# Four graph layers on one core: where an eigenproblem's last steps, a normalization pass and the first loads stand in the order of work

## The chip, the core and the metric

The kernel runs on one core of a Trainium2 chip. The core has five engines, each with its own queue of instructions, which it works off in order: TensorE (PE; its weight loads are listed apart as PEld), VectorE (DVE), ScalarE (ACT), GpSimd (POOL) and SyncE (SP), which here only issues DMAs. ScalarE and POOL issue some DMAs too. Engines wait for one another through semaphores. The metric is the device time of one execution in microseconds; lower is better.

## The reference

The input x is 128 graphs of 64 nodes with 256 features, in float32. Four layers follow, each as `x = layernorm(x + layer(x))`, and all with one 64 x 64 adjacency matrix.

```
layer 0: h = relu(adj @ (x @ Wg0 + bg0)); h = relu(adj @ (h @ Wg1 + bg1))
         for p in 1..4: LSTM over windows of p nodes, its last state replaces the window's last node
layer 1: A_hat = D^-1/2 (adj + I) D^-1/2; z = (A_hat @ x) @ W1.T + b1
         z = relu(batchnorm(z)); z = z @ W2.T + b2; batchnorm(z) over all 8192 nodes
layer 2: e = a . leaky_relu(Xq[src] + Xq[dst]) + log(adj[src,dst] + eps) for 512 edges, 4 heads
         softmax over the edges of each source node; Y[src] += attn * Xv[dst]; Y @ W_out.T
layer 3: _, U = eigh(L_norm(adj)); h = relu((U.T @ x) @ W1 + b1); U @ (h @ W2 + b2)
```

The eigenvectors U depend on the adjacency alone, so they can be worked out at any time before layer 3.

## The kernel before

**Data.** x stays in SBUF as the tile X: 64 blocks of 128 rows (two graphs) by 256. Products with the adjacency use a 128 x 128 matrix with the 64 x 64 one twice on its diagonal: `bda` (adjacency), `bdah` (layer 1's A_hat). Layer 3 writes its U and U transposed into these same two tiles (`bdu`, `bdut`), by `spread()` (L2014).

**The order of work.** The program is written with Python generators that yield between steps, so that one stage's steps can be traced between those of another (`run`, L1984). A planner then orders every engine's queue: it takes instructions by the order in which they were traced, as soon as its cost model has their inputs and memory ready, and so moves some of them forward or back.

**The eigenproblem** is done mostly on VectorE in small instructions, cut into pieces (`FastEigh.steps`, L1174): tridiagonalization of the 64 x 64 matrix (62 columns, five pieces each, L733), 30 implicit QL sweeps on four 16 x 16 leaves at once, postprocessing of the sweeps on tiles of 64 x 480, rotations, then two merges (32, then 64 wide), each with a bisection of 31 bits, and the products that give U and UT. Every piece yields a number, its price. `pump(n)` (L1363) adds n to what is owed, and issues pieces until their prices have used it up (a bare yield counts 2.6). It is called after every gate of the LSTMs with 0.8 or 1.6 x M/512 x PACE (M columns; PACE is 1.75, L1361), with 6 and 5 after each block of layer 1's two passes, and with `work[0]` after each step of layer 2's scores. Before layer 2 only the QL part must be done (L1751); the remaining pieces are issued after the scores (L2022).

**The general path.** The quick eigensolver flags cases that it can't treat in `bad`. A check (L2026, L2027) turns the flag into a count of 0 or 1, and a loop over that count (L2031) holds a slower, general solver. With these inputs the loop's body is skipped, but every engine loads the count into a register and branches. In the old order this stands between the scores and layer 3.

**Layer 0** takes four groups of 16 blocks of X. `convolve` (L1520) makes the two graph convolutions of a group; `windows` (L1559) the LSTMs for p = 1 to 4; `residual` (L1610) adds and normalizes. The steps of the next group's convolution and the last group's residual are traced between the gates. Loads: identity, adjacency and constants first (L1272 to L1278), x by `load_x` (four blocks of X a DMA), then weights and biases on ScalarE's queue (L1487 to L1501).

**Layer 1** passes three times over 16 quarters of four blocks. The first pass makes z and its statistics; the second the second product and its statistics, into Y; the last (`last_pass`, L1754) scales Y, transposes it back on TensorE, adds it to X and normalizes. The last pass is traced within layer 2's scores: four steps of it ahead, then one with each step of the scores.

**Layer 2.** `scores` has 32 steps of two blocks. A step holds, for each of two heads' halves c, four edge products (L1876), their copy by ScalarE (L1882) and leaky relu by VectorE (L1883), the products with `a` (L1829), and also the maps to Xq and Xv (L1853) of the next step and the transposes (L1842) of the one after. The 16 steps of a half fill one PSUM pair `sc`. Then `softmax` (L1897) works on it on VectorE, with one exponential on ScalarE, in seven steps; `table` (L1917) transposes the result and scatters it into `attn_d` in DRAM with four indirect DMAs on POOL; `fetch` (L1932) gathers it back as dense matrices `M2` with eight DMAs on SyncE. `values` (L1965) has 33 steps: load a block pair's table from M2 (`load`, ScalarE copy L1944, POOL fetch of Xv L1947), mix (L1959), map and normalize (L1980). Steps from the 16th on need the second table.

**Layer 3.** `blocks` (L2107) is a pipeline of four stages over 16 quarters: `basis` (L2071; it also adds a constant to X on POOL), `first_map`, `back` and `second_map` (L2098; it normalizes, and stores to the output from SyncE). It needs U and the quarter's X from the values.

Of the kernel before, what the change touches and what calls it, by code (L numbers as in the profile page):

```python
# [7 lines left out]
F32 = mybir.dt.float32  # L8
I32 = mybir.dt.int32
# [5 lines left out]
N = 64  # L15
NB = 128
D = 256
# [685 lines left out]
class FastEigh(Eigh):  # L703
# [29 lines left out]
    def tridiagonal(self, A0, QT, e, dcol):  # L733
# [12 lines left out]
        for i in range(N - 2):  # L746
# [11 lines left out]
            yield 1.2  # L758
            self.rsqrt(y, h)
            yield 1.2  # L760
# [12 lines left out]
            yield 1.2  # L773
            ps = self.ps(N)
            self.mm(ps, A, H)
            yield 1.2
# [4 lines left out]
            yield 1.2  # L781
# [478 lines left out]
def tile_adj_resnorm(ctx: ExitStack, tc: tile.TileContext, I: dict, out: bass.AP, layers: int = 4):  # L1260
# [5 lines left out]
    def load(name, shape, src, eng=nc.sync, dtype=F32):  # L1266
        t = const.tile(shape, dtype, tag=name, name=name)
        eng.dma_start(t, src)
        return t


    ident = load("ident", [P, P], I["ident"])  # L1272
    bda = const.tile([P, P], F32, tag="bda", name="bda")
    v.memset(bda, 0.0)
    for b in range(2):
        nc.sync.dma_start(bda[b * N : (b + 1) * N, b * N : (b + 1) * N], I["adjT"])
    adj = load("adj", [N, N], I["adj"], s)
    cst = load("cst", [N, CONST_COLS], I["consts"], nc.gpsimd)  # L1278
    X = const.tile([P, NT, D], F32, tag="X", name="X")
    xt = I["x"].rearrange("(t b) n d -> (b n) t d", b=2)  # L1280
    kio = lambda w: w.rearrange("(k p) f -> p k f", p=P)
# [35 lines left out]
    def psum(rows, w):  # L1317
        return eps.tile([P, 512], F32, tag="eps", name="eps")[:rows, :w]
# [42 lines left out]
    PACE = 1.75  # L1361
# [98 lines left out]
    with tc.tile_pool(name="lw", bufs=1) as lw, tc.tile_pool(  # L1460
# [10 lines left out]
        def load_x(g):  # L1471
            for q in range(TG // 4):
                t0 = g * TG + q * 4
                nc.sync.dma_start(X[:, t0 : t0 + 4, :], xt[:, t0 : t0 + 4, :])
# [12 lines left out]
        wg0 = lw.tile([P, 2, D], F32, tag="wg0", name="wg0")  # L1487
        s.dma_start(wg0, kio(I["Wg0"]))
        wg1 = lw.tile([P, 2, D], F32, tag="wg1", name="wg1")
        s.dma_start(wg1, kio(I["Wg1"]))  # L1490
        bl = lw.tile([P, 4, 8], F32, tag="bl", name="bl")
        bh = lw.tile([P, 4, 8], F32, tag="bh", name="bh")
        s.dma_start(bl, I["bih"])
        s.dma_start(bh, I["bhh"])
# [3 lines left out]
        b0c = lw.tile([P, 2], F32, tag="b0c", name="b0c")  # L1498
        s.dma_start(b0c, I["bg0"].rearrange("o (c p) -> p (o c)", p=P))
        b2c = lw.tile([P, D], F32, tag="b2c", name="b2c")  # L1500
        s.dma_start(b2c, I["bg1"].partition_broadcast(P).rearrange("p o d -> p (o d)"))  # L1501
# [249 lines left out]
    while not fast.ql_done:  # L1751
        next(pieces)

    def last_pass():  # L1754

        ln = Norm(nc, sy, X, 8, act=True)
        for q in range(NQ):
            y = sy.tile([P, 2, 512], F32, tag="y", name="y")
            for c in range(2):
                s.activation(y[:, c, :], Y[:, q, c, :], AF.Identity,  # L1760
                             bias=sh2[:, c : c + 1], scale=sc2[:, c : c + 1])
            for j in range(0, 4, 2):
                ps = pp.tile([P, 512], F32, tag="m", name="m")
                for i in range(2):
                    for c in range(2):
                        te.transpose(ps[:, i * D + c * P : i * D + (c + 1) * P], y[:, c, (j + i) * P : (j + i + 1) * P], ident)
                ln.add(q * 4 + j, ps, 2)
            yield

    only1.close()  # L1770
    qlp.close()
    own.close()
    sy = own1(keep1, name="l1z", bufs=2)
# [4 lines left out]
    with ExitStack() as l2:  # L1778
# [7 lines left out]
        fast.psum, fast.bank = pp, "m"  # L1786
# [24 lines left out]
        taken, late, work = [], [], [3.5]  # L1811
# [24 lines left out]
        def transposed(k):  # L1836

            xT = []
            for t in (2 * k, 2 * k + 1):
                ps = pp.tile([P, 512], F32, tag="m", name="m")  # L1840
                for c in range(2):
                    te.transpose(ps[:, c * P : (c + 1) * P], X[:, t, c * P : (c + 1) * P], ident)  # L1842
                xT.append(sx.tile([P, 2, P], F32, tag="xT", name="xT"))
                v.tensor_copy(xT[-1].rearrange("p c n -> p (c n)"), ps[:, :D])  # L1844
            return xT

        def maps(k, xT):

            xq, xv = [], sx.tile([P, 2, D], F32, tag="xv", name="xv")
            for i in range(2):  # L1850
                ps = pp.tile([P, 512], F32, tag="m", name="m")
                for c in range(2):
                    te.matmul(ps, xT[i][:, c, :], wqv[:, c, :], start=(c == 0), stop=(c == 1))  # L1853
                xq.append(sx.tile([P, D], F32, tag="xq", name="xq", bufs=4))
                taken.append(s.copy(xq[i], ps[:, :D]))
                s.copy(xv[:, i, :], ps[:, D:])
            nc.sync.dma_start(xvd[k], xv)
            return xq

        def scores():  # L1860
# [8 lines left out]
            for k in range(K):  # L1869
                xn = None  # L1870
                for c in range(2):
# [17 lines left out]
                    if c == 1 and k < K - 2:  # L1889
                        xT = transposed(k + 2)  # L1890
                xq = xn
                pump(work[0])
# [91 lines left out]
        def run(*steps):  # L1984
            for x in steps:
                next(x, None)

        bank = None
        sc_, p3 = scores(), last_pass()
        run(*[p3] * 4)  # L1990
        work[0] = 0.0
        run(*[sc_, p3] * (NQ - 4))
        for _ in p3:
            pass
        keep1.close()
        lw, sm = own1(valuing, name="l2w", bufs=1), own1(valuing, name="l2s", bufs=2)
# [3 lines left out]
        run(*[sc_] * (HU - NQ + 4))  # L2000
        for _ in range(3):
            run(sc_, soft[0], soft[0])
        run(soft[0])
        work[0] = 4.5
        run(sc_)
# [3 lines left out]
        run(*[sc_] * 7)  # L2009
        run(sc_, val, sc_, sc_, val, sc_)  # L2010
        scoring.close()


        def spread():  # L2014
            for bd, m in ((bdu, U), (bdut, UT)):
                for b in range(2):
                    r = slice(b * N, (b + 1) * N)
                    v.tensor_copy(bd[r, r], m[r, :])

        with tc.tile_pool(name="eps3", bufs=1, space=PSUM) as eps:  # L2020
            fast.psum, fast.bank = eps, "eps"
            for _ in pieces:  # L2022
                pass
            again = ek.tile([1, 1], I32, tag="again", name="again")
            ps = psum(1, 1)
            te.matmul(ps, fast.bad, ones[:N, 0:1], start=True, stop=True)  # L2026
            v.tensor_scalar(again, ps, 0.0, None, ALU.is_gt)  # L2027
            for bd in (bdu, bdut):
                v.memset(bd, 0.0)
            spread()  # L2030
            with tc.For_i(0, nc.values_load(again[0:1, 0:1], min_val=0, max_val=1)):  # L2031
                with tc.tile_pool(name="gk2", bufs=1) as gk2, tc.tile_pool(name="gt2", bufs=1) as gt2, tc.tile_pool(
                    name="gp2", bufs=1, space=PSUM
                ) as gp2:
                    Eigh(tc, gk2, gt2, gp2, cst, ident, ones).from_leaves(*fast.state, U, UT)
                spread()
# [4 lines left out]
        with tc.tile_pool(name="l3w", bufs=1) as l3w, tc.tile_pool(name="l3s", bufs=2) as s3, tc.tile_pool(  # L2041
# [75 lines left out]
            run(val, soft[1], val, soft[1], soft[1], val, soft[1], val, soft[1], soft[1], val)  # L2117
            table(es[1])
            run(val)
            constants()  # L2120
            run(val)
            fetch(1)
            run(*[val] * 7)

            run(*[val, val, l3, val, l3] * 5)
# [64 lines left out]
```

## Time and profile before

| | us |
|---|---|
| median of three runs | 2501.85 (2501.39 to 2501.97) |
| profiled execution | 2496.09 |
| its span, first to last instruction | 2494.2 |
| TensorE busy | 2292.2 |
| VectorE busy | 1796.8 |
| ScalarE busy | 952.6 |
| layer 0's first convolution starts at | 23.7 |
| layer 0's last LSTM matmul ends at about | 1507 |
| layer 1's second pass ends on TensorE at | 1796.8 |
| last score product ends at | 2224.0 |
| the loop's register loads at | 2269.9 |
| second table landed at | 2331.9 |

The profile shows one execution; its span is what its instructions cover. Times in it are counted from its first instruction. In rows of groups, a line is `line engine operation output<-inputs shapes xcount | busy, mean ns | idle before it and what ended that`. L numbers are those of the code before. The helper lines L117 to L148 are the eigenproblem's small instructions. "Granted clock" is the share of full speed that TensorE's clock had.

### The profile page before, as it was taken

To read this page: it belongs to the slowest core of one execution; us is meant where nothing else is said; L and a number is where in the kernel's file an instruction comes from. 1 tells how busy PE (TensorE), PEld (TensorE's weight loads), DVE (VectorE), ACT (ScalarE), POOL (GpSimd) and SP (SyncE) were. 2 spreads that over 40 slices of the span, in tenths; PEclk is the share of its full clock that TensorE was granted. 3 is DMA by queue.
4 is the path that set the end of the run, shared out by engine and by line. 5 is a ranking of instruction groups with operands and counts; after the bars stand their busy time and mean duration, and the time that the engine had idled before them with its cause. 6 is when DMAs were issued, how large, how long until landed. Compare 5 with 4: busy or idle time off the path is not lost. (4 is left out here: it accounts for less than half of the span.)

```text
span 2494.2 us, 29191 instructions
## 1 busy us (share of the span) xinstructions
PE 2292.2 (92%) x9016; PEld 1225.4 (49%) x9016; DVE 1796.8 (72%) x8156; ACT 952.6 (38%) x1635; POOL 76.3 (3%) x115
## 2 busy tenths in 40 slices
PE   6999999999999999999999997989889888965797
PEld 4544654444664445655446544544433322324697
DVE  3566655677677798777888777877866676886477
ACT  1233222333222333222433222334366654544575
POOL 0000000000000000000000000000000000001232
PEclk9999999999999999999999998999999999987899
DMA  6000000001000001000101000022100005002522
GB/s 211 18 17 34 1 34 1 34 34 51 1 34 1 34 34 51 1 34 1 51 17 51 35 1 34 1 97 85 51 30 21 17 26 97 22 30 58 104 82 85
DMA packets 59859, 101.24 MB, mean 41 GB/s; under 512 B 5136, under 2 KB 40080, under 8 KB 59440
## 3 DMA queue, kind: packets, MB, share of 16 engines
q1 hardware_dynamic: 54304, 88.39, 10.9%
q0 software_dynamic: 3216, 10.21, 1.4%
q8 instruction: 72, 1.18, 0.2%
q10 hardware_dynamic: 2176, 0.72, 0.1%
q14 instruction: 91, 0.75, 0.1%
HBM read 67.84 MB, written 31.46 MB: 40 GB/s over the span
## 5 line engine op out<-in xcount | busy, mean ns | idle before, releaser
L1583 PE MATMUL pq<-H,wi 128*128 128x512 f32 (+1 forms) x2016 | 827.6, 546 | 3.8 <-DVE H L1608 3.8
L1589 ACT ACTIVATE gate<-pq,bl 128x512 f32<-128x512 f32 (+1 forms) x504 | 318.4, 635 | 835.8 <-PE pq L1587 651.2
L1583 PEld LDWEIGHTS pq<-H,wi 128*128 128x128 f32 x2016 | 372.0, 190 | 329.8 <-issue 260.2
L1587 PE MATMUL pq<-lh,wh 128*128 128x512 f32 (+1 forms) x1152 | 467.4, 533 | 14.8 <-DVE lh L1604 14.1
L1587 PEld LDWEIGHTS pq<-lh,wh 128*128 128x128 f32 x1152 | 215.5, 190 | 215.9 <-issue 141.0
L1883 DVE SCALAR_TENSOR_TENSOR xs<-xs 128x512 f32<-128x512 f32 x256 | 166.0, 681 | 84.1 <-ACT xs L1882 83.8
L1882 ACT COPY xs<-l 128x512 f32<-128x512 f32 x256 | 137.3, 589 | 108.9 <-PE l L1876 56.0
L1876 PE MATMUL l<-edge_s,xq 64*128 64x512 f32 x512 | 138.2, 657 | 24.1 <-ACT xs L1882 12.4
L1853 PE MATMUL m<-wqv,xT 128*128 128x512 f32 x256 | 126.0, 621 | 1.9 <-DVE xT L1844 1.9
L1729 PE MATMUL ps<-at,w 128*128 128x512 f32 x256 | 117.2, 610 | 9.9 <-ACT at L1725 8.8
L1746 PE MATMUL ps<-h,w 128*128 128x512 f32 x256 | 112.1, 600 | 8.8 <-ACT h L1741 8.8
L142 DVE COPY AQR<-eps 64x192 f32<-64x192 f32 (+1 forms) x125 | 35.1, 280 | 118.1 <-PE eps L148 117.9
L1253 ACT ACTIVATE X<-X,ln_sh,ln_rs 128x256 f32<-128x256 f32 x192 | 98.6, 589 | 36.6 <-DVE ln_sh L1249 28.6
L1601 ACT ACTIVATE gate<-lc 128x1024 f32<-128x1024 f32 (+1 forms) x72 | 69.0, 958 | 102.3 <-DVE lc L1596 52.2
L1237 DVE BATCH_NORM_STATS2 ln_st<-X 128x6 f32<-128x256 f32 x256 | 97.9, 413 | 1.5
L1876 PEld LDWEIGHTS l<-edge_s,xq 64*128 64x128 f32 x512 | 47.0, 196 | 84.5 <-issue 35.8
L1746 PEld LDWEIGHTS ps<-h,w 128*128 128x128 f32 x256 | 49.0, 193 | 70.4 <-issue 57.5
L1947 POOL DMA_DIRECT2D xr<-xv x32 | 17.6, 550 | 2088.2 <-DVE xs L1883 1823.4
L1729 PEld LDWEIGHTS ps<-at,w 128*128 128x128 f32 x256 | 47.9, 193 | 67.1 <-issue 49.4
L1853 PEld LDWEIGHTS m<-wqv,xT 128*128 128x128 f32 x256 | 45.4, 194 | 71.0 <-issue 57.5
L1234 DVE TENSOR_TENSOR X<-ps,X 128x512 f32<-128x512 f32 x63 | 42.8, 680 | 46.8 <-PE ps L1980 32.1
L1598 DVE TENSOR_TENSOR gate<-gate 128x1024 f32<-128x1024 f32 (+1 forms) x36 | 38.1, 1058 | 52.5 <-ACT gate L1589 52.4
(558 smaller groups left out, 3228.3 us busy)
## 6 DMA issues: line engine op xcount, KB each, us to landing
wi<-in_WihT_dram SPq DMA_DIRECT2D x16, 1024.0 KB, 4.8
wh<-in_WhhT_dram SPq DMA_DIRECT2D x12, 1024.0 KB, 6.9
X<-in_x_dram SPq DMA_DIRECT2D x16, 512.0 KB, 8.5
xd<-X SPq DMA_DIRECT2D x16, 512.0 KB, 2.6
X<-xd SPq DMA_DIRECT2D x16, 512.0 KB, 3.2
xv<-xv SPq DMA_DIRECT2D x32, 256.0 KB, 2.0
xr<-xv POOLq DMA_DIRECT2D x32, 256.0 KB, 2.9
M<-attn_d SPq DMA_DIRECT2D x16, 512.0 KB, 11.6
```

The lines of the kernel that those rows point to most:

```text
L1237: nc.vector.bn_stats(st, self.X[:, k, :])
L1253: nc.scalar.activation(x, x, AF.Identity, bias=sh[:, k : k + 1], scale=rs[:, k : k + 1])
L1583: te.matmul(ps, wi[:, kk, o * P : (o + 1) * P], at(kk, k), start=(kk == 0), stop=(k == 0 and kk == 1))
L1587: te.matmul(ps, wh[:, kk, o * P : (o + 1) * P], hst[:, kk, :M], start=False, stop=(kk == 1))
L1589: s.activation(gates[gt][:, c, :M], ps, AF.Tanh if gt == 2 else AF.Sigmoid, bias=bl[:, p - 1, o : o + 1])
L1601: s.activation(gg, cs2, AF.Tanh)
L1729: te.matmul(ps, w1[:, k, c * P : (c + 1) * P], at[:, k, :], start=(k == 0), stop=(k == 1))
L1746: te.matmul(ps, w2[:, k, c * P : (c + 1) * P], h[:, k, :], start=(k == 0), stop=(k == 3))
L1853: te.matmul(ps, xT[i][:, c, :], wqv[:, c, :], start=(c == 0), stop=(c == 1))
L1876: mms.append(te.matmul(pl[i][:, b, :], xq[i][r, c * P : (c + 1) * P], GG[r, :], start=True, stop=True))
L1882: taken.append(s.copy(x, pl[i][:, b, :]))
L1883: ready.append(v.scalar_tensor_tensor(x, x, 0.2, x, ALU.mult, ALU.max))
```

## The change

1. The general path's check and loop, with `spread`, move from behind the scores to behind layer 1's second pass, ahead of the last pass and of layer 2. All remaining pieces are now issued before it (`for _ in pieces`). So that fewer remain, PACE is 1.9 and all five of the tridiagonalization's pieces are priced 1.1 (the first row of the diff, five times). The scores no longer pump pieces.
2. The last pass works in half quarters (two blocks), normalizes four blocks at once instead of eight, and is stepped from within `scores`, twice a step. Four half quarters are traced ahead of the scores.
3. `transposed` uses one PSUM tile and one SBUF tile (a single buffer) for both blocks of a step.
4. Seven steps of the values are traced with the last seven steps of the scores (before: two in the last six). Layer 3's blocks are traced from the second softmax on, between its steps and those of the values; before, from 16 steps of the values on.
5. The adjacency halves go on two queues. b0c, Wg0 and X's first four blocks are traced next, identity and adj move to ScalarE's queue, and layer 0's other weights and biases follow; they live in a pool of their own.

```diff
-            yield 1.2
+            yield 1.1
...
-    ident = load("ident", [P, P], I["ident"])
     v.memset(bda, 0.0)
     for b in range(2):
-        nc.sync.dma_start(bda[b * N : (b + 1) * N, b * N : (b + 1) * N], I["adjT"])
-    adj = load("adj", [N, N], I["adj"], s)
-    cst = load("cst", [N, CONST_COLS], I["consts"], nc.gpsimd)
+        (nc.sync, s)[b].dma_start(bda[b * N : (b + 1) * N, b * N : (b + 1) * N], I["adjT"])
+    head = ExitStack()
+    lh = head.enter_context(tc.tile_pool(name="lh", bufs=1, side="right"))
+    s.dma_start(b0c, I["bg0"].rearrange("o (c p) -> p (o c)", p=P))
+    nc.sync.dma_start(wg0, kio(I["Wg0"]))
+    nc.sync.dma_start(X[:, :4, :], xt[:, :4, :])
+    ident = load("ident", [P, P], I["ident"], s)
+    adj = load("adj", [N, N], I["adj"], s)
+    nc.sync.dma_start(wg1, kio(I["Wg1"]))
+    s.dma_start(b2c, I["bg1"].partition_broadcast(P).rearrange("p o d -> p (o d)"))
+    s.dma_start(bl, I["bih"])
+    s.dma_start(bh, I["bhh"])
+    cst = load("cst", [N, CONST_COLS], I["consts"], nc.gpsimd)
-    PACE = 1.75
+    PACE = 1.9
-    while not fast.ql_done:
-        next(pieces)
+    for _ in pieces:
+        pass
     def last_pass():
-        ln = Norm(nc, sy, X, 8, act=True)
+        ln = Norm(nc, sy, X, 4, act=True)
         for q in range(NQ):
-            y = sy.tile([P, 2, 512], F32, tag="y", name="y")
-            for c in range(2):
-                s.activation(y[:, c, :], Y[:, q, c, :], AF.Identity, ...)
             for j in range(0, 4, 2):
+                y = sy.tile([P, 2, 2 * P], F32, tag="y", name="y")
+                for c in range(2):
+                    s.activation(y[:, c, :], Y[:, q, c, j * P : (j + 2) * P], AF.Identity, ...)
...
                 ln.add(q * 4 + j, ps, 2)
-            yield
+                yield
     own.close()
+    def spread():
...
+    with tc.tile_pool(name="eps3", bufs=1, space=PSUM) as eps:
+        again = ek.tile([1, 1], I32, tag="again", name="again")
+        ps = psum(1, 1)
+        te.matmul(ps, fast.bad, ones[:N, 0:1], start=True, stop=True)
+        v.tensor_scalar(again, ps, 0.0, None, ALU.is_gt)
+        for bd in (bdu, bdut):
+            v.memset(bd, 0.0)
+        spread()
+        with tc.For_i(0, nc.values_load(again[0:1, 0:1], min_val=0, max_val=1)):
+            ...
-    sy = own1(keep1, name="l1z", bufs=2)
+    sy = own1(keep1, name="l1z", bufs=3)
         def transposed(k):
-            for t in (2 * k, 2 * k + 1):
-                ps = pp.tile([P, 512], F32, tag="m", name="m")
...
-                xT.append(sx.tile([P, 2, P], F32, tag="xT", name="xT"))
-                v.tensor_copy(xT[-1].rearrange("p c n -> p (c n)"), ps[:, :D])
+            ps = pp.tile([P, 512], F32, tag="m", name="m")
...
+            xT = sx.tile([P, 2, 2, P], F32, tag="xT", name="xT", bufs=1)
+            v.tensor_copy(xT.rearrange("p i c n -> p (i c n)"), ps)
         def scores():
...
                         xT = transposed(k + 2)
+                    next(beside[0], None)
                 xq = xn
-                pump(work[0])
-        run(*[p3] * 4)
-        run(*[sc_, p3] * (NQ - 4))
+        run(*beside * 4)
+        run(*[sc_] * (NQ - 2))
...
-        run(*[sc_] * 7)
-        run(sc_, val, sc_, sc_, val, sc_)
+        run(*[sc_] * 4)
+        run(*[sc_, val] * 7)
         scoring.close()
...
             l3 = blocks()
-            run(val, soft[1], val, soft[1], soft[1], val, soft[1], val, soft[1], soft[1], val)
+            constants()
+            run(val, soft[1], val, soft[1], l3, soft[1], val, soft[1], l3, soft[1], val, soft[1], l3)
             table(es[1])
-            run(val)
-            constants()
-            run(val)
+            run(val, l3)
             fetch(1)
-            run(*[val] * 7)
-            run(*[val, val, l3, val, l3] * 5)
+            run(*[val, val, l3] * 10)
             run(*[val] * 2, *[l3] * (NT // 4))
```

## The prediction

> **What bounds the kernel now.** I read the page first, then its stages as windows, then the chain that ended last, then the timeline at the start and where TensorE stood still.
>
> ```profile
> span 2494.2 us, 29191 instructions
> PE 2292.2 (92%) x9016; PEld 1225.4 (49%) x9016; DVE 1796.8 (72%) x8156; ACT 952.6 (38%) x1635; POOL 76.3 (3%) x115
> ...
> PE   6999999999999999999999997989889888965797
> ```
>
> The page's first rows and its TensorE row in 40 slices: TensorE is full except in the first slice, somewhat in the scores (slices 29 to 35), and in slices 35 to 37. A change can win only there; elsewhere it can only push work against a full engine. Windows size the stages (columns: length, then PE, PEld, DVE, ACT, POOL busy, granted clock, DMA share):
>
> ```profile
> 1235.00:1319.00 84.00, 79.67 (x198) 36.01 (x197) 75.50 (x394) 28.30 (x38) 0.00 (x0) 0.98 0.07 26
> 1831.00:1995.00 164.00, 147.40 (x632) 56.05 (x630) 110.91 (x277) 105.84 (x218) 1.09 (x2) 0.95 0.06 23
> 2004.00:2025.00 21.00, 20.51 (x90) 6.95 (x90) 12.41 (x22) 11.18 (x24) 0.00 (x0) 1.00 0.04 14
> 2224.00:2273.00 49.00, 3.41 (x14) 2.02 (x14) 40.12 (x135) 1.26 (x2) 0.00 (x0) 0.53 0.01 2
> 2273.00:2333.00 60.00, 44.12 (x516) 35.34 (x516) 33.08 (x127) 40.04 (x81) 10.56 (x16) 0.90 0.68 140
> 2333.00:2481.00 148.00, 146.22 (x1404) 134.24 (x1405) 108.15 (x368) 96.75 (x202) 51.65 (x77) 0.98 0.20 68
> ```
>
> In order: layer 0 with VectorE at 75.5 of 84; scores beside the last pass; scores alone; the eigenproblem's tail, where TensorE works 3.4 of 49 us; the values until the second attention table is back; values and layer 3's blocks, TensorE-bound (146 of 148). A 13 us tail follows. The idle tail by TensorE's own account:
>
> ```profile
> 2256.03 0.28 PE L183 MATMUL eps<-ident,delta 64*64 64x64 f32 x1 [32.06 <-DVE mid L117]
> ```
>
> It waited 32 us for VectorE's bisection. Then the chain that ended last, the second table's way through DRAM:
>
> ```profile
> 2289.07 1.76 ACT at L1925 x2
> ...
> 2299.92 2.46 DMA attn_d<-at,edge_s
> ...
> 2320.46 11.45 DMA M<-attn_d
> ...
> 2332.15 1.06 ACT mc L1944
> ```
>
> From the table's transposes (2287.4) to its landing (2331.9) is 44.5 us; table 0 took 41.8 (2078.2 to 2120.0). Lastly the start:
>
> ```profile
> 14.38 0.39 ACTq L1488 DMA_DIRECT2D wg<-in_Wg_dram  x1
> ...
> 21.48 0.28 DVE L1509 TENSOR_SCALAR b0w<-ones,b0c 128x128 f32<-128x128 f32 x1
> ...
> 23.70 2.61 PE L1527 MATMUL ps<-bda,X 128*128 128x128 f32 x16
> ```
>
> The first convolution waits behind weights that ScalarE's queue issued only at 14.4 us, though the first X block had landed at 9.4.
>
> **The change part by part.** Gains are minus.
>
> *Loads first: -11 (-14 to -6).* The adjacency halves go out on two queues (one landed at 3.9 us, the second at 7.6), b0c and Wg0 with them, X[:4] third on SyncE. Three issues at 0.4 to 0.6 us, about 4 us to land and the bandwidth of the X blocks (1.35 us each) put X at 8 to 9. Ahead on TensorE stand the degree matmuls, at 11.8 and 13.9 in the trace, some 3.7 us earlier with the adjacency. So the convolution starts at 9 to 15, I take 11 (-12.7), less 2 because its evacuations now share VectorE with the edge sort. ScalarE's queue carries seven issues (about 3.7 us); its first work was at 9.2, so they hide.
>
> *Pace 1.9 for 1.75, tridiagonal yields 1.1 for 1.2: +12 (+3 to +25).* A gate pumps 0.8 or 1.6 x M/512 x PACE; the four windows sum to 19.2 + 35.2 + 39.9 + 43.2 = 137.5 per group, 550 for four: 962 units before, 1045 after. Layer 1 adds 16 x 6 + 16 x 5 = 176. The pieces' yields sum to 1220 before (tridiagonal 62 x 5 x 1.2 = 372), 1189 after (341). So before 1220 - 1138 = about 80 units, the 64-merge, were left for the scores and the tail; after, 1221 exceeds 1189 and the last piece goes out about block 9 of layer 1's second pass. The tail vanishes, but 113 units more run in layer 0: the QL's end (5), its postprocessing (21), rotations (52), last pair (8) and part of the 32-merge (28). A unit is about 1 us of VectorE (70.7 us of pieces for 69.8 units in the last group's third window). Most hides under matmuls. Where VectorE is 75.5 of 84, +8.6% on 58 us of pieces is 5 us more and perhaps 3 of it shows, twice; the postprocessing (480-wide operations of 0.65 us, which cost nothing in layer 1) lands in the third window, 77 of 93 busy: 6 more. Sum 12. Layer 1 stays TensorE-bound (9.03 us a block).
>
> *General loop after the second pass: -2 (-6 to +5).* It brings its check, two memsets, four small copies, a register load on all five engines and the branch. Before, TensorE stood 3.5 us (2269.5 to 2273.0), ScalarE until a table load ended at 2276.4, 6.5 us. It now stands before the last pass, which needs ScalarE first: +6. SyncE's and POOL's queues cross the branch too; the weights had been fetched at 1652, and even issued behind it they are wanted 10 us later. Against that, the normalization chain loses the merge's operations between its own (-2), and two quarter-blocks of last pass stand before the scores instead of four (11 us from first y to first X: -6).
>
> *Last pass in halves, two per score step: -8 (-18 to +4).* Twelve steps with it took 164 us, 13.7 each; alone 10.36 by the stores' distance; its eight transposes add 1.33 of TensorE: ideal 11.7. Here a rule and the rows part. Every second step had a thin stretch of 2.6 us of TensorE idle in bits of 0.5 to 0.8, and each time a granted clock of 0.5 for 3.41 us followed (mean 0.95 in the window). The Trainium skill, "TensorE: Matmul & The Clock Gate", section "HAM oscillation — how this bites in real kernels", asks only for no idle gap over about 3.4 us: by it these gaps cost their 2.4 us beyond the usual, six times, 14 us. By the row each costs half of 3.41 more, 24 us in all; I use the row. Normalizing 4 blocks for 8 halves the burst on ScalarE, but costs: 32 wide activations become 64 narrow (2 x 0.505 - 0.76 = 0.25 each, 8 us ScalarE), eight more flushes (1 us VectorE each). Both hide: ScalarE 106, VectorE 111 of 164. The single xT buffer makes its copy wait for the maps' matmuls, queued before it anyway; score operations stand behind that copy. I take 12.6 per step, midway between ideal and present: 14 steps 176 against 164 + 2 x 10.4 = 185.
>
> *Pieces gone from the late scores: -3.* Steps of 11.5 to 12.1 beside pieces return to 10.4. The stall for table 0 (11.7 us) stays.
>
> *Seven values in the scores: +17 (+10 to +22).* Each is 2.83 us TensorE (0.91 + 1.92), 2.75 ScalarE, 2.3 VectorE, one table copy and one POOL fetch; 7 x 3.0 with PSUM's two shared banks, less the 4 us that four mixes already cost.
>
> So the scores end at 2224 - 11 + 12 - 2 - 8 - 3 + 17 = 2229.
>
> *From the scores' end.* The softmax, which hid under the merge (2223 to 2245), is exposed: 21 us alone; values and blocks put up to 11 us of VectorE among it. A rule speaks against this: blocks add on POOL (four of 0.725 us each), and "GPSIMD Engine Reference", section "8. Key points", says POOL contends with VectorE operations of two SBUF inputs. Two answers:
>
> ```profile
> L1217 DVE SCALAR_TENSOR_TENSOR is_r<-is_r,is_s 128x8 f32<-128x8 f32 x6 | 1.0, 166 | 0.2
> ```
>
> ```profile
> L1217 DVE SCALAR_TENSOR_TENSOR is_r<-is_r,is_s 128x4 f32<-128x4 f32 x20 | 8.4, 421 | 0.4
> ```
>
> The first is beside the last pass, the second beside POOL's adds: 0.25 us per operation. Twelve softmax operations times that is 3; by the rule as total exclusion all 12 adds would count, 8.7. I take 2, as not all meet: 26 us (21 to 33). The table then takes 43 us (40 to 48). A store of 512 KB may stand before its gather on SyncE, waiting for a block's norm, about as long as the scatter does anyway. So 69 us pass; TensorE has for them nine values (25) and five blocks, filling (1.8 + 3.6 + 4.5 + 6.2 + 6.2 = 22): some 20 us of waiting are late next.
> After the landing it took 162 us before; 22 us of blocks are done by then: 140.
>
> End: 2229 + 26 + 43 + 140 = **2438** against the span of 2494.2 (execution 2496.1). The median 2501.85 lies 7.65 above the span; with that, **2446**.
>
> **Rivals.** *More (2422, 0.15):* layer 0 absorbs the pieces (-9), the last pass nears 11.8 a step (-11), table latency 39 (-4). For it: VectorE 70 to 90% busy, not full. Against: it is in order.
> *Less (2474, 0.17):* the last pass gains nothing (+8), layer 0 pays 20 (+8), SyncE's stores hold the gather and the softmax queues (+12).
> *Slower (2515, 0.05):* VectorE becomes layer 0's bound. All 113 moved units unabsorbed would give 2446 - 12 + 113 = 2547; it decides from 68 of 113 unabsorbed. The 84 us window speaks for it; the second group's, with 67 of 90, against.
> *Nothing (2502, 0.03):* the planner puts the blocks late, so that TensorE waits the 49 us in the table's shadow.
>
> **How the numbers follow.** The forecast has 0.60, its own range 2430 to 2462. To leave out two in ten at most I reach to 2418 and 2480. This kernel can tell about 0.2%, 5 us: faster 0.92, same 0.03, slower 0.05.
>
> **What would show it.** First L1527 matmul near 11 us; layer 0's windows up to 8 us longer where VectorE is fullest; no pieces after 1770; the register load before the last pass; score steps near 12.6 without clock dips; no 32 us wait; one wait of about 20 us for the second table. Wrong if the scores end after 2250, or the table needs over 80 us from there.

## The result, and the profile after

The changed kernel takes 2470.69 us in the median of four runs (2466.12 to 2471.62), against 2501.91 us for the kernel before (2501.39 to 2504.48). The ratio is 0.987, with a 95% interval from 0.9852 to 0.9887: 31 us less. The forecast was 2446 with a range from 2418 to 2480.

The page of the changed kernel, its first rows and TensorE's row in 40 slices:

```profile
span 2469.8 us, 29195 instructions
...
PE 2300.6 (93%) x9016; PEld 1232.0 (50%) x9016; DVE 1794.5 (73%) x8172; ACT 964.4 (39%) x1678; POOL 75.1 (3%) x115
...
PE   7999999999999999999999988998978888899797
```

Counted from 0, slices 35 to 37 showed 6, 5, 7 before and show 9, 9, 7 now; the scores (slices 30 to 34) show 8 throughout. The span fell by 24.4 us, from 2494.2. Windows of the changed kernel, chosen as those of before (length, then PE, PEld, DVE, ACT, POOL busy, granted clock, DMA share): layer 0's fullest window, scores beside the last pass, the softmax, the second table's way, and the rest.

```profile
1246.50:1332.50 86.00, 80.53 (x198) 36.42 (x197) 77.02 (x413) 28.13 (x38) 0.00 (x0) 0.96 0.07 26
1845.00:2009.00 164.00, 139.18 (x624) 54.21 (x623) 114.41 (x300) 115.81 (x253) 1.09 (x2) 0.97 0.06 23
2256.00:2291.00 35.00, 29.08 (x274) 26.29 (x274) 29.92 (x64) 22.24 (x38) 13.49 (x19) 0.90 0.16 44
2291.00:2334.00 43.00, 34.45 (x330) 30.73 (x328) 26.16 (x100) 26.52 (x57) 13.08 (x18) 0.86 0.86 166
2334.00:2460.00 126.00, 120.36 (x1176) 107.06 (x1176) 93.37 (x334) 83.95 (x176) 34.93 (x53) 0.97 0.24 75
```

The second row is the surprise: in 164 us of scores beside the last pass TensorE now works 139 us, where it worked 147 before, with almost as many products (624 for 632). At the higher clock (0.97 for 0.95) they take less time, and TensorE stands 25 us instead of 17. The 49 us in which it had all but stood still for the bisection (3.4 us of work) are gone; from the scores' end to the table's landing it works 63.5 of 78 us.

Stage by stage, each length from the instructions' times in the two traces:

| stage | before | after | change | forecast |
|---|---|---|---|---|
| start to the first convolution matmul | 23.7 | 18.9 | -4.8 | -11 |
| from there to layer 0's last LSTM matmul | 1483.3 | 1505.9 | +22.6 | +12 |
| layer 1's two passes | 289.8 | 289.9 | +0.1 | 0 |
| second pass's end to the 16th step's store of Xv | 217.3 | 221.3 | +4.0 | -10 |
| from there to the last score product | 209.9 | 220.0 | +10.1 | +14 |
| to the second table's last transposes | 64.1 | 34.3 | -29.8 | -38 |
| from these to the table's landing | 43.8 | 43.9 | +0.1 | -1 |
| landing to the end | 162.3 | 135.6 | -26.7 | -22 |

The changes sum to -24.4. Three rows carry the 32 us by which the forecast span of 2438 was too low: the last pass (14 us), layer 0 (11), and the softmax (8); the loads' 6 us are made up by the last row and the score row.

### The profile page after: what moved, and what is told of

It is laid out like the page before. It is cut to its first block, busy times and chain, and to the rows that moved or that the text cites. A ratio compares the mean times of both kernels' runs of the same rounds, so it can differ in the third digit from the quotient of the medians.

```text
span 2469.8 us, 29195 instructions
## 1 busy us (share of the span) xinstructions
PE 2300.6 (93%) x9016; PEld 1232.0 (50%) x9016; DVE 1794.5 (73%) x8172; ACT 964.4 (39%) x1678; POOL 75.1 (3%) x115
## 5 line engine op out<-in xcount | busy, mean ns | idle before, releaser
L1591 PE MATMUL pq<-lh,wh 128*128 128x512 f32 (+1 forms) x1152 | 474.8, 538 | 24.9 <-DVE lh L1608 24.6
L1857 PE MATMUL sc<-xs,az 128*32 128x512 f32 x512 | 68.2, 605 | 3.0 <-DVE xs L1910 3.0
```

The lines of the kernel that those rows point to most:

```text
L1591: te.matmul(ps, wh[:, kk, o * P : (o + 1) * P], hst[:, kk, :M], start=False, stop=(kk == 1))
L1857: mms.append(te.matmul(sc[half][c][q : q + 32, :], az[:, c, HU - 1 - u_ : 3 * HU - 1 - u_], xs[b, i], start=(u_ == 0), stop=(u_ == HU - 1)))
```

## Experiments

**Parts of the change, each alone.** Three kernels are the kernel before with one part each. The first takes over the order of the first loads only (part 5 of the change, its diff as shown above).

> The kernel before with the order of the first loads alone changed. The forecast's step: the first convolution starts near 11 us instead of 23.7 and the time falls by 11 us (6 to 14). Rival, from the changed kernel's trace: the identity, now third on ScalarE's queue, lands at 9.0 us, the degree chain on VectorE waits for it, and the first convolution stands behind that chain on TensorE; then it starts near 19 us and the time falls by about 5 us.

2498.53 us, ratio 0.9988 (0.9979 to 0.9997): 3 us less. The timeline of this kernel:

```profile
8.51 0.29 DVE L1343 TENSOR_TENSOR jk<-bda,ident 128x128 f32<-128x128 f32 x1 [2.62 <-DMA ident<-in_ident_dram]
...
11.73 0.19 DVE L1503 TENSOR_TENSOR bl<-bl,bh 128x32 f32<-128x32 f32 x1 [0.55 <-DMA bh<-in_bhh_dram]
...
19.17 3.10 PE L1531 MATMUL ps<-bda,X 128*128 128x128 f32 x16
```

The rival holds in its mechanism, though the time falls by 3 us rather than 5: VectorE's degree chain waits for the identity, now third on ScalarE's queue, and the convolution comes at 19.2. The second line shows a further load in the same queue, layer 0's biases (bh). It costs 0.55 us here; the last experiment shows what it costs when the identity is early.

The second kernel takes over the pieces' pace only.

```diff
-            yield 1.2
+            yield 1.1
...
-    PACE = 1.75
+    PACE = 1.9
```

> The kernel before with the pace 1.9 and the tridiagonalization's price 1.1 alone. Both theories: nothing of the eigenproblem is left behind layer 1's second pass, the scores lose their pieces (-3 to -5), and the way from the last score product to the second table's transposes falls from 63 us to about 30 (softmax 26, loop 3.5), -33. The forecast: layer 0 grows by 12 us, so about -25 in all. Rival: layer 0 grows by 22 us, as it does in the changed kernel, by recurrent gate products that wait for VectorE, so about -15. If layer 0 grows by clearly less than 22, another part of the change (the loads' order or pools) has its share in it.

2482.45 us, ratio 0.9921 (0.9903 to 0.994): 19 us less. The groups of recurrent gate products, on the pages of before and of this kernel (busy, mean ns of one, idle before it and what ended that):

```profile
L1587 PE MATMUL pq<-lh,wh 128*128 128x512 f32 (+1 forms) x1152 | 467.4, 533 | 14.8 <-DVE lh L1604 14.1
```

```profile
L1587 PE MATMUL pq<-lh,wh 128*128 128x512 f32 (+1 forms) x1152 | 474.8, 538 | 25.0 <-DVE lh L1604 24.7
```

Layer 0's sixteen windows (an LSTM of one p for one group each) are, within 0.2 us each, those of the changed kernel, so its whole +22 us belongs to the pace. The recurrent products wait 10 us more for VectorE's hidden states and are 7 us longer themselves. Half of the 22 us, 11.5, falls in the first group, which the tridiagonalization fills with 282 small matmuls of the eigenproblem instead of 240 (70.1 us for 59.9). In the second group there are 42 fewer, but only 0.6 us comes back: in its third window VectorE is now busy 116 of 118.5 us, and recurrent products wait 5.0 us for it there.

The same kernel says what the pace buys. From the last score product to the second table's last transposes it takes 34.0 us, against 64.1 before and 34.3 in the changed kernel, with the loop still in its old place: it is the pace alone that empties the tail.

The third takes over the last pass in halves with its single transposed tile (part 2 and 3).

```diff
-        ln = Norm(nc, sy, X, 8, act=True)
+        ln = Norm(nc, sy, X, 4, act=True)
...
+                    next(beside[0], None)
...
-        run(*[sc_, p3] * (NQ - 4))
+        run(*[sc_] * (NQ - 2))
```

> The kernel before with the last pass in half quarters, twice a step, with its single transposed tile, alone. The forecast: 12.6 us a step, 14 steps, -8 us. Rival, from the changed kernel's trace: each step has one stop of TensorE of 1.95 us, in which ScalarE runs four normalizations ahead of the copies that free PSUM; mean step 13.7 with a clock dip each fourth, and 14 such steps instead of 12: +4 to +9 us.

2506.63 us, ratio 1.002 (1.0013 to 1.0027): this part alone makes the kernel 5 us slower. A step takes 13.72 us over 14 steps (192.0 us between stores), no less than before (13.68 over 12). From the second pass's end to the 16th step's store it needs 223.5 us, against 221.3 in the changed kernel; what the moved loop and the absent pieces save there is the 2.2 us between them. The halves and the single transposed tile were not run apart.

If the parts add up (pace -19, loads -3, halves +5), the rest of the change, the loop, the values and the blocks together, is worth about 15 of the 31 us.

**What stops the step.** Before, TensorE's idle time beside the last pass (groups of the kernel before, 1835 to 1985 us) was spread over several waits; the two largest rows:

```profile
L1876 PE MATMUL l<-edge_s,xq 64*128 64x512 f32 x182 | 53.4, 712 | 5.1 <-ACT xq L1855 5.1
...
L1766 PE MATMUL m<-ident,y 128*128 128x128 f32 x90 | 14.5, 282 | 7.0 <-DVE X L1234 3.9 <-DVE xT L1844 2.6
```

In the changed kernel's groups of TensorE, 1850 to 2000 us, it stands in one place:

```profile
L1903 PE MATMUL l<-edge_s,xq 64*128 64x512 f32 x176 | 48.1, 669 | 1.3
L1880 PE MATMUL m<-wqv,xT 128*128 128x512 f32 x88 | 40.7, 605 | 0.0
L1770 PE MATMUL m<-ident,y 128*128 128x128 f32 x88 | 14.4, 287 | 21.4 <-ACT xv L1883 21.4
```

The last pass's transposes need a PSUM bank that the maps fill and ScalarE's copies of Xq and Xv empty. One step of its timeline says why those are late:

```profile
1893.78 3.70 PE L1880 MATMUL m<-wqv,xT 128*128 128x512 f32 x8
...
1896.78 2.07 ACT L1253 ACTIVATE X<-X,ln_sh,ln_rs 128x256 f32<-128x256 f32 x4 [0.54 <-DVE ln_sh L1249]
1898.76 0.35 ACT L1882 COPY xq<-m 128x256 f32<-128x256 f32 x1
1899.01 0.36 ACT L1883 COPY xv<-m 128x256 f32<-128x256 f32 x1
...
1899.43 0.66 PE L1770 MATMUL m<-ident,y 128*128 128x128 f32 x4 [1.95 <-ACT xv L1883]
```

Four normalizations of 0.5 us run ahead of the copies. Two kernels change this, each from the changed kernel: one gives the normalization to VectorE, the other leaves it on ScalarE and puts it off by half a step.

```diff
-        ln = Norm(nc, sy, X, 4, act=True)
+        ln = Norm(nc, sy, X, 4)
```

> The changed kernel with the last pass's four normalizing operations a step on VectorE instead of ScalarE. If ScalarE's burst ahead of the copies is what stops TensorE (1.95 us a step, and the clock dips with it), the step falls from 13.7 to about 11.5 and the time by about 30 us. If the step is bound by TensorE's own work, or the dips come without the stops, it stays at 13 or more and the time moves by less than 8. If VectorE (9.5 us of 13.3 a step, and about 1.5 more here) becomes the limit, it lands between, with stops that VectorE ends.

2434.31 us, ratio 0.9729 (0.9711 to 0.9747): 36 us below the changed kernel. Windows of this kernel:

```profile
1844.10:2008.10 164.00, 161.97 (x764) 64.89 (x761) 151.72 (x399) 107.44 (x240) 1.09 (x2) 1.00 0.08 28
```

TensorE works 162 of 164 us at a clock of 1.00, and each step takes 11.20 us. VectorE carries 152 of 164 and doesn't limit it: one normalization there takes 407 ns.

```profile
L1255 DVE TENSOR_SCALAR X<-X,ln_mv,ln_rs 128x256 f32<-128x256 f32 x55 | 19.0, 407 | 0.0
```

```diff
-        ln = Norm(nc, sy, X, 4, act=True)
+        ln = Norm(nc, sy, X, 8, act=True)
...
+                if len(ln.todo) == 4:
+                    ln.flush()
                 y = sy.tile([P, 2, 2 * P], F32, tag="y", name="y")
...
```

> The changed kernel with the last pass's normalization put off by half a step, so that it stands behind the next maps' first copies on ScalarE's queue; the amount of work is the same. If the place of the four operations ahead of the copies stops TensorE, the step falls from 13.7 to 11.2 to 11.8 us and the time by 25 to 35 us, as with the normalization on VectorE. If ScalarE's load as such is the limit (9.6 us of 13.3), the step stays above 12.5 and the time falls by less than 15.

2458.12 us, ratio 0.983 (0.9814 to 0.9847): 12.6 us less than the changed kernel, below the 25 to 35 of the first theory and, with a step of 12.53 us, within the second's. The clock stays full. The groups show that the stop only moved:

```profile
L1907 PE MATMUL l<-edge_s,xq 64*128 64x512 f32 x192 | 47.9, 615 | 17.6 <-ACT xq L1886 16.2
L1884 PE MATMUL m<-wqv,xT 128*128 128x512 f32 x96 | 44.4, 605 | 0.0
L1772 PE MATMUL m<-ident,y 128*128 128x128 f32 x96 | 14.4, 273 | 0.0
```

The planner put three of the four normalizations between the two pairs of copies, so the first bank came free and the next edge products waited for the second Xq, 1.35 us a step. By the numbers set in advance this is the second theory's outcome, ScalarE's load. The timelines speak for the place in the queue all the same. In the changed kernel the maps had filled the first bank at 1895.8 us, and ScalarE stood idle for the 0.54 us up to 1896.78 with the copies queued behind the burst; here it stands idle for 0.60 just ahead of the burst, and the stop has moved with the burst. But no run keeps the four operations on ScalarE without a stop, so no experiment tells place and load apart. That the four operations on ScalarE are what stops TensorE is shown by the kernel that has them on VectorE.

**The table's shadow.** Here the changed kernel traces layer 3's blocks only from the 16th step of the values on.

```diff
-            run(val, soft[1], val, soft[1], l3, soft[1], val, soft[1], l3, soft[1], val, soft[1], l3)
+            run(val, soft[1], val, soft[1], soft[1], val, soft[1], soft[1], val, soft[1])
             table(es[1])
-            run(val, l3)
+            run(val)
             fetch(1)
-            run(*[val, val, l3] * 10)
+            run(*[val] * 4)
+            run(*[val, val, l3, val, l3] * 5)
```

> The changed kernel with layer 3's blocks traced only from the 16th step of the values on, as in the old order; the seven values in the scores and all else as changed. The forecast's sum: 22 us of blocks no longer fill the table's way, softmax and table come 3 to 8 us earlier without them, so +14 to +19 us. Rival: what TensorE does in the table's shadow isn't what sets the end, and the time moves by less than 5. The softmax, 34 us in the changed kernel: if the blocks' POOL additions stretch VectorE's operations, it falls to about 26; if the values' own VectorE work does, it stays above 30.

2494.63 us, ratio 0.9973 (0.9964 to 0.9983): 24 us more than the changed kernel. TensorE's wait for the second table, 9.7 us in the changed kernel, is the timeline's

```profile
2331.21 3.05 PE L1986 MATMUL m<-mc,xr 64*64 64x64 f32 x60 [23.50 <-ACT mc L1971]
```

and another of 12.9 us stands before the table's transposes. The blocks are what fills the shadow. The transposes still come 30.5 us behind the last score product, against 34.3: without any POOL addition beside it the softmax is hardly shorter, and VectorE works 28.1 of those 30.5 us.

**Waits at the first table.** From here on each kernel builds on the one with the normalization on VectorE. In that kernel TensorE stops 10.0 us where the first table lands, as it did in the two compared kernels (11.7 us before, 9.4 after). This one holds the first two table copies back.

```diff
-            s.copy(m.rearrange("p c i h n -> p (c i h) n"), ...)
+            cp = s.copy(m.rearrange("p c i h n -> p (c i h) n"), ...)
+            if k < 2:
+                after(cp, taken[-1:], mybir.DependencyClass.NoSync)
```

> The kernel with the normalization on VectorE (2434 us) and the first two table copies of the values held behind the last score copies traced before them on ScalarE. If the 9 us stop of TensorE at the first table's landing (and the clock dip behind it) is that copy standing too early in ScalarE's queue, both go: -9 to -12 us, about 2424. If the landing itself is what the next steps need, the stop moves to the first mix and the time stays within 4.

2433.45 us (0.973): nothing gained beyond noise, though not by the reason given. The timeline of this kernel:

```profile
2103.81 0.37 ACT L1883 COPY xv<-m 128x256 f32<-128x256 f32 x1 [6.99 <-DMA xv<-xv]
...
2104.24 0.65 PE L1869 MATMUL m<-ident,X 128*128 128x128 f32 x4 [3.06 <-ACT xv L1883]
```

The table copy is out of the way, and a second wait stood behind it: ScalarE's copy into one of two Xv tiles waits for the store of the tile's former content, which SyncE issued only after the table's eight gathers. The next kernel issues those stores on POOL.

```diff
-            nc.sync.dma_start(xvd[k], xv)
+            (nc.sync if k < HU else nc.gpsimd).dma_start(xvd[k], xv)
```

> As the kernel with the held table copies (2433 us), with the Xv stores of the scores' second half issued by POOL instead of SyncE. There the stop at the first table had only moved: ScalarE's copy of Xv waited 7.0 us for a store that stood behind the table's eight gathers on SyncE. If that queue is the last wait at this place, the steps around the first table run at 10.2 us, the clock dip behind it goes too, and the time falls by 5 to 9 us, to about 2426. If another wait stands behind this one, or POOL's scatter holds the stores, it stays within 3.

2425.92 us, ratio 0.97 (0.9684 to 0.9717): 7.5 us less. The steps around the first table run at 10.2 us, with no stop over 1.2 us.

**Values out of the scores.** A first try, on the kernel with VectorE's normalization, only cut the count.

```diff
-        run(*[sc_] * 4)
-        run(*[sc_, val] * 7)
+        run(*[sc_] * 7)
+        run(*[sc_, val] * 4)
```

> The kernel with the normalization on VectorE (2434 us) and four values in the scores instead of seven. The forecast priced a value in the scores at 2.4 us of TensorE; the second table's way through DRAM still leaves TensorE about 10 us idle in one piece. If the moved values fill that, the scores end 6 to 12 us earlier and the time falls by 4 to 9. If VectorE, full in the softmax (34 us of 34), is what sets the table's landing, the three values queue in front of it there, and the time is the same or up to 6 longer.

2489.04 us, and it says nothing on its question: the three calls were not made up for later, so this kernel leaves out the values' last two steps, and layer 3's blocks follow right behind the values that they need. Its group of first block products shows what that costs:

```profile
L2074 PE MATMUL ps<-bda,X 128*128 128x128 f32 x238 | 53.3, 400 | 52.2 <-ACT X L1253 52.2
```

They waited for the normalization of their own quarter, 4.0 us at most blocks, where the changed kernel's wait 0.6 us in all. Blocks need a lead of values. The mended form, with the same count in the scores, on the kernel with the stores on POOL:

```diff
-            run(val, soft[1], val, soft[1], l3, soft[1], val, soft[1], l3, soft[1], val, soft[1], l3)
+            run(val, soft[1], val, soft[1], soft[1], val, soft[1], soft[1], val, soft[1])
             table(es[1])
             run(val, l3)
             fetch(1)
-            run(*[val, val, l3] * 10)
+            run(val, l3, val, val, l3, val, l3, val, val, l3)
+            run(*[val, val, l3] * 9)
```

> As the kernel with the Xv stores on POOL, with four values in the scores instead of seven, no blocks traced within the softmax, and the three values and five blocks traced behind the second table's scatter. By VectorE's sum the softmax was 34 us because values' and blocks' work stood between its operations, and TensorE had about 15 us idle in the table's shadow. If so, the scores end 7 us earlier, the second table's transposes come 28 to 31 us behind them, and the time falls by 6 to 10 us. If TensorE has too much left when the table lands, or the scatter waits on POOL behind fetches of Xv, the gain is under 3 us.

2419.58 us, ratio 0.9677 (0.9661 to 0.9693): 6.3 us less again, and the fastest kernel here, 51 us below the changed one. Windows of this kernel, the softmax and the table's way:

```profile
2200.00:2233.00 33.00, 17.96 (x181) 14.97 (x182) 29.67 (x66) 19.19 (x32) 5.81 (x8) 0.84 0.15 47
2233.00:2281.00 48.00, 46.30 (x491) 41.16 (x490) 24.38 (x80) 29.71 (x61) 19.58 (x28) 0.90 0.78 154
```

The scores end 11 us earlier (2200.0 for 2211.0). The softmax, 32.5 us, is still longer than expected, although no block is traced in it (the planner still moved one quarter's four POOL additions there): VectorE is busy 29.7 of 33 us, most of it with the softmax and the values. TensorE stands 15 us in it and works 46 of 48 us in the table's shadow.

**Pace and loads, once more.** One kernel moves pieces from layer 0 to layer 1, on the kernel with the stores on POOL (all five prices 1.2 again).

```diff
-            yield 1.1
+            yield 1.2
...
-    PACE = 1.9
+    PACE = 1.85
...
-        pump(6)
+        pump(7)
...
-        pump(5)
+        pump(6)
```

> As the kernel with the Xv stores on POOL, with the tridiagonalization's price back at 1.2, the pace at 1.85 and 7 and 6 instead of 6 and 5 pumped after each block of layer 1's passes: 1017 units in layer 0 instead of 1045, 208 in layer 1, for 1220 in all. The 22 us that layer 0 paid came half from its first group, where the tridiagonalization ran 18% denser and now runs 6% denser than in the kernel before. If they follow the density of the pieces, layer 0 falls by about 10 us and layer 1, with VectorE busy for 199 of 272 us, hides the rest: -7 to -10. If layer 1's second pass gets full on VectorE, it gives back 3 to 8 of it.

2430.1 us (0.9715): 4 us more. Layer 0 ended 13.1 us earlier (1510.7 for 1523.8), better than expected. But layer 1 gave back 7 us, and the merge's last transposes on TensorE ended at 1817.8, behind the second pass instead of within it, so that the scores ended 5 us later. The pieces' prices do not say when a chain of dependent operations is done.

The last puts the identity and the adjacency first on their queues, on the fastest kernel.

```diff
+    ident = load("ident", [P, P], I["ident"])
+    adj = load("adj", [N, N], I["adj"], s)
     bda = const.tile([P, P], F32, tag="bda", name="bda")
...
-    ident = load("ident", [P, P], I["ident"], s)
-    adj = load("adj", [N, N], I["adj"], s)
```

> As the kernel with values and blocks in the table's shadow (2420 us), with the identity and the adjacency issued first again, each at the head of its queue, and the adjacency halves, b0c, Wg0 and X behind them. If the first convolution stands behind the degree chain, and that chain behind the identity's landing (9.0 us in the changed kernel), the chain starts at 5.5 to 6.5 us, the first convolution at 15 to 16.5 instead of 18.9, and the time falls by 2 to 4 us, about what three rounds can tell. If X or the weights come later than that behind the two more loads, the convolution starts at 18 or later and nothing is gained.

2422.01 us (0.9686), no gain. The timeline of this kernel:

```profile
5.38 0.28 DVE L1343 TENSOR_TENSOR jk<-bda,ident 128x128 f32<-128x128 f32 x1
...
12.67 0.19 DVE L1503 TENSOR_TENSOR bl<-bl,bh 128x32 f32<-128x32 f32 x1 [5.89 <-DMA bh<-in_bhh_dram]
...
20.43 3.01 PE L1531 MATMUL ps<-bda,X 128*128 128x128 f32 x16
```

The identity is there at 5.4 us, and VectorE then stands 5.9 us for the biases, an addition that nobody needs yet and that stands in the middle of the degree chain. Both loads gated the start in turn. Issuing the biases later was not tried.

## Why the prediction was right, and where it was not

The direction and the range held. The likeliest case did not: 2470.7 lies outside its own range of 2430 to 2462 and beside the rival "Less" (2474), whose three reasons (nothing gained in the last pass, a dearer layer 0, a longer way of the second table) are, in part, what happened. One mark set in advance fell: the scores end at 2256.0, after 2250. The other held narrowly: the table lands 78 us later, not over 80.

1. **Loads first, -11: measured -4.8.** The step that failed is "some 3.7 us earlier with the adjacency". The adjacency came only 1.2 us earlier (first used at 6.4 for 7.6), and the degree matmuls 1.7 us later (13.5 and 15.6 for 11.8 and 13.9). The chain also reads the identity, which the change moved from the head of SyncE's queue to the third place on ScalarE's, and a bias addition that came to stand in it. I followed one operand where the instruction has two, and one queue where the engine had other work in it.

2. **Pace, +12: measured +22.6,** inside its range of 3 to 25. The mechanism, recurrent gates waiting for VectorE, was right, and the windows that the sum did price, at 3, 3 and 6 us, measured 3.2, 2.0 and 1.9. The mis-sized term is the first group, 11.5 us, for which the sum had nothing: the tridiagonalization grew by 18.4% there (price and pace together), not by 8.6%, and its matmuls sit on TensorE, the full engine. Some of the 22.6 is the one execution of the kernel before: with the same pieces, layer 0 took 1485.8 us in the kernel with the halves alone and 1489.8 in the one with the loads alone, for 1483.3.

3. **Loop after the second pass, -2:** the difference between the halves alone and the changed kernel is 2.2 us, which includes the absent pieces and loads. Nothing in it contradicts the step, but the loop was not moved alone in any run.

4. **Last pass in halves, -8: it costs.** This is the step that failed most, by 14 us together with the boundary. "Normalizing 4 blocks for 8 halves the burst on ScalarE" is true, 2.07 us for 4.04, but a burst now comes in every step, and each one still stands ahead of the copies that free TensorE's PSUM banks: a stop of 1.95 us a step. The cover named for it, ScalarE with 106 of 164 us busy, was an average, and says nothing of what stands ahead of the copies. "Midway between ideal and present" had no mechanism behind it. The ideal, 11.7, was even pessimistic: VectorE's normalization gives 11.20.

5. **Gaps and the clock.** The row was the better guide than the rule here. The Trainium skill, "TensorE: Matmul & The Clock Gate", section "HAM oscillation — how this bites in real kernels", asks for no idle gap over about 3.4 us. The changed kernel's last pass has none over 1.95, and still the mean clock of every fourth step fell to 0.89, which made it 1.65 us longer. The row was misread in one point: the window shows five dips, not six. The section on the hardware, below, has what the traces say on when a dip comes.

6. **Pieces gone from the late scores, -3; seven values, +17.** The pace alone makes that stage 4.3 us shorter (205.6 for 209.9) and the halves alone 2.8 (207.1); the changed kernel's +10.1 then leaves about 17 for the values, if the parts add up, which is what was forecast.

7. **Softmax, 26: measured 34.3,** above its range of 21 to 33. The sum listed 21 us of its own and up to 11 of values and blocks on the same engine, and then took 26. VectorE works in order and was busy 29.9 of 35 us: the two had to be added. The POOL rule (the Trainium skill, "GPSIMD Engine Reference", section "8. Key points") was rightly weighed low: beside the blocks' additions a few operations stretched (one scan 1.60 us for 1.21), and without the blocks the stage lost 3.8 us, with their own VectorE work in it.

8. **Table, 43: 43.9. After the landing, 140: 135.6.** The chain that ended last shows the store that I had named on SyncE:

```profile
2305.32 2.08 ACT X L1253 x4
2307.40 0.10 ACT is_s L1214
2307.50 0.32 SPq L2103
2307.82 0.04 issue
2307.86 0.58 SPq L1964
...
2309.63 2.07 SPq L1964
...
2321.92 12.24 DMA M<-attn_d
2335.37 1.61 PE m L1986 x32
```

A block's store (L2103) waited for its normalization between the first gather (L1964) and the second, which was issued 2.3 us behind the first, and with it the others behind. "One wait of about 20 us" became one of 9.7 and two of 2.8 and 2.9: TensorE found 63.5 us of work in these 78 us, where the sum had 47 in 69. Filling was worth 24 us.

The offset of 7.65 us between span and median, added at the end, belonged to that one execution: the changed kernel's median lies 0.9 above its span. The kernel before, timed 31 times beside the first four experiments, runs from 2496.5 to 2506.0; its profiled execution (2496.1) was faster than all of these. That is why the medians differ by 31 us and the spans by 24. The offset brought the forecast some 7 us nearer to the median; that was luck.

## What to carry to other kernels

Halving a burst does not help if it stays ahead of the same copies in an in-order queue: look for what stands ahead of the instruction that frees the waiting engine's buffer, and move that work to an engine with slack. When a wait is removed, read the next one in the same place before pricing the gain; here one load hid another behind it, and a table copy hid a store. Where extra work is put beside a serial stage on the same engine, add the two.

## What the hardware showed unexpectedly

The granted clock dipped without long gaps. A stop of 1.95 us in each 13.3 us step brought a dip in every fourth step; 2.6 us in bits in every second step, before, brought one in five of six; 1.47 us in each 12.5 us step, with the normalization put off, brought none in thirteen steps.

The clock records of the traces say more. Within an execution the clock changes only at instants that lie a multiple of 3.41 us apart, so the span can be cut into slots of that length. In all fourteen traces, counting only slots at full clock, each of the 162 in which TensorE was idle for more than 2.1 us was followed by a slot at half clock. Of the 9186 with under 1.5 us of idle time 11 were, all of them between 80 and 95 us from the start. In between it was 64 of 140. So in these runs it is the idle time summed in a slot that counts, whether in one piece or in bits, and the border lies at about half of the slot. Two slots with their successors, in the changed kernel's last pass:

```profile
1881.56:1884.97 3.41, 1.47 (x7) 0.59 (x5) 0.87 (x3) 3.11 (x8) 0.00 (x0) 1.00 0.00 0
1884.97:1888.38 3.41, 3.41 (x10) 1.19 (x8) 2.13 (x6) 2.20 (x5) 0.00 (x0) 0.50 0.20 77
...
1908.86:1912.27 3.41, 1.90 (x5) 0.57 (x3) 1.69 (x6) 2.87 (x7) 0.00 (x0) 1.00 0.00 0
1912.27:1915.69 3.42, 2.99 (x20) 1.26 (x20) 2.26 (x6) 3.00 (x8) 0.00 (x0) 1.00 0.20 77
```

In the first the whole stop falls into one slot (1.47 of 3.41 us busy), and the next slot has half the clock; in the third row the stop is cut in two by the slots' border, and no dip follows. Steps of 13.3 us drift against the slots, so that the stop falls whole, or nearly so, into one in about every fourth step; at 1867.9 and 1922.5 us, with 1.94 and 1.90 us idle, it brought no dip, so the border is not sharp. A stop of 1.35 us stays under the border wherever it falls.

A 16 KB load took 4.8 us in the kernel before (half of the biases, issued at 15.9 us, landed at 20.7) and 8.9 us in the last experiment (3.7 to 12.6), where it was issued beside X's first blocks and most of the other loads. Whether it is their number or their size that delays it was not tested.

Layer 0's windows differ in clock between executions of the same instructions: its last window took 94.3 us at a clock of 1.00 in the kernel before, 97.1 at 0.97 in the kernel with the loads alone and 96.8 at 0.97 in the one with the halves alone, with the same pieces in it. A few us of a single execution's time are of this kind.
